# A recorded four-layer kernel played in another order: new tables of issue order, copy engines and buffer places

## The chip, the cores and the metric

The kernel runs on one core of a Trainium2 chip as one program. The metric is the device time of one execution in microseconds (us), as the median of several runs. The engines are TensorE (PE, matrix products; its weight loads are listed as PEld), VectorE (DVE), ScalarE (ACT), GpSimd (POOL) and SyncE (SP, which issues plain transfers). Each works through its own instructions strictly in order and waits for the others at semaphores.

## The reference

The input `x` is 2 batches x 1024 tokens x 128 channels in float32. Four layers follow, and each does the same around two functions of its own:

```python
xn = _layernorm(x, axis=-1)
s = _L0_attn_ref(xn, ...)
g = _silu(_L0_ffn_ref(xn, ...))
x = x + s * g          # then layers 1, 2 and 3 in the same way
```

- Layer 0: a delta rule in chunks of 32 tokens (a recurrence over a state, `next` in the kernel), two causal convolutions of `v` with 7 and 25 taps (`local`, `mid`, made of `conv` operations), and a router that mixes four such outputs (`mixed`); the other function is a chain of ternary linear maps with gelu.
- Layer 1: attention of 16 heads over all 1024 tokens, with a score made from distances (`sim`, `e`, `av`); the other function is a mixture of 8 experts of which each token uses 2.
- Layer 2: linear attention with 16 heads of 64; the other is a small transformer block on the eighth of the tokens that a router picks.
- Layer 3: causal attention of 16 heads with one shared key and value; the other is two blocks of attention in windows of 64 tokens with a gated map behind each (`g`, `a`, `u`, `down`).

## The kernel before

The stage functions (`l0_attn` L802, `l0_ffn` L1139, `l1_attn` L1171, `l1_ffn` L1335, `l2_attn` L1514, `l2_ffn` L1616, `l3_attn` L1823, `l3_ffn` L1982) do not issue anything. Their calls go to a recorder (`Record`, `note` and `product`, L472-L545), for layer after layer and batch after batch (`program`, L2234). The recorder makes 6,968 *units*, numbered in the order of recording. A unit is one operation of DVE, ACT, POOL or SP, or up to 32 matrix products of one tile shape on PE. Each unit knows which units must come before it. Copies that empty a PSUM bank (`evac`, L703) may run on ACT or on DVE; there are 426.

When all is recorded, `Record.order` (L547) decodes the table `ORDER` (from L308): a permutation of the unit numbers, with one bit in each that says whether a copy goes to DVE. `Record.issue` (L563) plays the units in that order. Each unit goes to the end of its engine's instruction stream, so the table fixes the order on every engine, PE's and the transfers' included. Where a unit first touches a tile, the tile gets a buffer: the next byte of the table `PLACES` says which place of its pool. There are 35 places of 128x1048 (`halves`, used by arrays such as `pr`, `mixed`, `xn`, and by the experts' weights `we`), 21 of 128x512 (`t512`, used by `e`, `xg`, `q`, `k`), 14 small ones, and 8 PSUM banks. A tile that takes a place waits until the last user of the tile before it is done. The two tables were computed elsewhere; the constants beside them (`LOAD`, `SHIFT`, `SEEN`) and the costs in `note` and `product` are not used when the kernel is built, except to give a unit its engine.

All engine calls are made on one line:

```python
for u, e in order:
    for b in u.buffers:
        if b.real is None:
            b.real = b.make(None if b.bufs is None else next(places))
    for op, args, kw in u.ops:
        if op == "evac":
            op = "copy" if e == ACT else "tensor_copy"
        f = getattr(engines[e], op)
        tc.keep_in_program_order(f(*map(real, args), **{k: real(v) for k, v in kw.items()}))
```

That is why every row of the profile says L584; groups are told apart by the names of their tiles.

The experts of layer 1 (L1335 and on, `gather` L1446, `fetch` L1455) need a word more. For each batch, tokens are sorted by expert into 23 tiles of 128 rows. POOL gathers the rows of each tile by an indirect transfer (`xg<-xd,token`), four tiles to a place of `t512`, and the expert's weights of each tile by another (`we<-in_experts,expert`), one to a place of `halves`. PE transposes the four parts of an `xg` (`tr<-const,xg`), multiplies by the weights (`up`, gelu on ACT, `down`), and POOL gathers the results back into token order (`y0`, `y1`). The indices `token`, `expert` and `slots` come from DVE.

Of the kernel before, what the change touches and what calls it, by code (L numbers as in the profile page):

```python
# [22 lines left out]
X = mybir.AxisListType.X  # L23
PSUM = bass.MemoryType.PSUM

P = 128
NB = 2
L = 1024
T = NB * L
# [240 lines left out]
def pack_inputs(inputs):  # L270
# [29 lines left out]
PE, ACT, DVE, POOL, SP = range(5)  # L300
# [8 lines left out]
    "c-nPZ2VfLM_rEu@ySI0jo)AJpOMuWJ0RjQ(h|(2l0s@~3A6?|bO3MK@M6rNMl@5Y{g@Ay7G=U%piF86q2%#h){qAymJM*8}-7Dey{-@q;nR)Z(z2AH9_a?"  # L309
    "5XIS2uSKb9`c`U3zksDRNK^2`Hx5c?p7VD>EbJpA)qTt37;Iv)RgK?#7{{11B!1HSGdg%;xImrnn54;sdYl>&s6J61Fsw+foMV&Le|hIgzLP`fnxOnls)L"  # L310
    "5pB`(D|G2GMkwE_>Xqw06}1`U62nTwzv#U9>3EP-p-2^b45g>i-I12q$GR{Ip0p5?<_EP%Z?Ughvj~qoER&;fyzT_lsIb&!o$hm<f9~vE`$DQ4)CxR{QsZ"
    "nZT|-N$|jZtxo{h(cN^aO32sgc(cbkr&`%W0#Eucgf1!Q(D<I}xeR7YOkB0Q$N4|u((O_G}M&&}1=UEVY<LA!~9)ZCrDN^?njqZB3z{+V3SpRND>I-0VeQ"
    "SN=+fgw4)9+@e9$EB!7IHaZ@(SB4suM!$hP*Kq9zgow7Vwt*A=5T9I+id0fPdew-RlUz%|x%hcPm;mceGzEH-Q_@Z&qJzbOp5pxZL7eQ@9{E1BfaDh$se!"
    "EsRY)3UT7KfsX*9pC@~vBokT#SWmPY3OoO9yKU6aWk*MWbg1{%(dzcm2T~#lz=4K|&=1!93t$<*OR`|C3RyWS2=#{-6S5B|dzT)lyApPx`Cncp?{8rXHM$"
    "V|)4|W*LI<+p$Ae_bH|tu!rSTac9iC}^{jN}FEu1UJeE+w8OzrgO0%$QF4t`m`M$s4ZAnVPZqxfzb-{9Y(M+DT}1Baxq(d_5oWS65wP4NBL+sIt8bk^7KP"
    "VDVQP*D);nZ2at4d>&;`T#$oq3|1X(4E|Pd?O~PE}S4V5=tVeFtLXF$*T9CtVx7FamUSL;6&F!dtl0U9L9TM^6F$q^~7WcKr^V9`!o~|^=4m#e>Uz8^a*!"
    ")Y}@BwX?_j5j!r(m(=)Pd8%T<r1ZyT}1HQw%=&-GV3P);ostR_900Kannvx}U0XW^+Gjd8~c?h(;86O02zMTu?GXfFn&zVuR{Eb40b{2x!UF+*<bzpkfl&"
    "Ym;rM2(W&gu&AFEwQN)<p|l!&BZFo&s-9XaV=?LaxnK8%l}e^DlHPGdSFkJdL0;oSZR@L&IF>Ftds~uF!e6**~oq9_l4NfJ$U_TA?%qT}-~1%m#(g0;>v7"
    "B7vcUBC7-bi4TUX)>)>MbHFep0g-+SYY%4uYL~e@QDqTvn4%u=!)U>=e!~9#P-2tq*7Elxvx>~{9+5Cn1v5(xf<wR{FhgMMHKp4lWwjPar4>1C0BH2jLYe"
    "kl8u(K=Ad!+$$Ya|!40a9OTIW6pxo?r5*xT?5Y=w$EBmfc3&apq6OKqYX4}g#2%%RYaBG`l!5MdN-9StyfCEe))D>%%VNyoBD^QCWgUor6|*aTyCxZ#!O-"  # L320
    "pLt%gh1IraoLexeC3@m)X;4k9yz+rOpF!0*-a%}3R6k<>4mf=qRl2+0S2bSxbPgQ4xv?;mP%pDGCc#1GkfS4vzBrRQ)2`bJ&K+?N1&9tVxgeE1K<h70-^="
    "*-ltTRs4S?TzokZ&M$!^9wNMYGc-v%502M_cx?*U}C*c-Ad36TEW?3m<0UL^u%p^O4iGWmBu-Ymp_zwa-9*2~(wXGh7890=r+YkmqT^$7T=?*Hx8yk!O2S"
    "E7UPmys|Cr^A~7t~wK)^yr1d-_t&F^f$gFy?D`V|^8($Z2(kvwf6=3bVc>Ws(IUq0$0m$7oDkQdB9y5d?@EIc&rVm_7jrEd)q~k9+huYK}yRIsrNUX)EGz"
    "mSH1GH+6!hq0nb1QS0Z`$q_MO=m^G8X`v(pIlxM=Lm&@pjfPjY{8}7|w)Qofk(<=Lr^Z8ptIwYIzw5KxA`1?6$cEmBh_j9$ta<-rB7xYP6gQkIsEsJbRe("
    "HEOk-LSDHKC6cMGN-9ENWtpj#35n&(8YUGaZszkaJNoQK}X>{6|w3gMexFC-C2ExQUHc&3b@i#dYhl~}l*LX`|ikwAU-3lhWP8io*38HVUIyi{aPc{X*9)"
    "gwBX3Dp4r1#>=$#AUsY(XUuC%_xHNr#t=jSxkP!PrHV~i(8>4JX+Ml)%zqm49$K!*_H-NC!k&46=%H!^Y6oct6d+Wv*san&*1Oxd^jaP9n6*R)iKy%0r(l"
    "tc*dV_x{KiJej`e+yRCP{rtiLbrd6t7=`tkeTs;hCN?3w{6@W|MVgbPPRV@zjjrw=ep>acq`Ai@bh2$Y1pPXR1k*OQ?=o9$k!DyR2Jrt>nks_4I^Glh19J"
    "LrI-T@f0``w5VaMgPtzz5{QhtL>DJ6VF53}1nIxj|HA2t0Xb*t3&X3V@omhAjsKk`h%Gv|#&ERqTr_4<>I#LA?$>f6!&w(mR|u<%YKtuQa(Id#AxeR3&*>"
    "P9m^w`^!_yg&vYamB;LaBhWKFvWoVUp)aB#<9i?Gz5;v-w`c}&Cm6+W23H|W1x(sNCT1B4{%#9r#QoiDh;64b7&m}hl`^<HUl54Hf<pKALk}Se1>LXxkj0"
    "_M0wo$AGY3Mp6v?(PKM1K3s3*9}13^ed8z(dHKM7;0>Pcu>EytStf3g#9joA6p!$;YZHbp+}oB1FqGm9a<iU+$YnK2m#KZrzNA~3bFOsKk|(6O$V9)l(bw"  # L330
    "Y=2w0%C4s`3ICJX7o}pTU~6?a>*0K%!>h~KnALeG=m~N4ym$M)`7bJnyxUoMKj#N;}CE{3}Z);9*WF_-cKsZOUnEf-fA>yzJuiv1i=WYK~NB_I)e!<i?#g"
    "TO+>$UdsqVsSO_$Odu0(&teRP5dn9V9QeM-d{zs2GX1fQ0NHHil?h)H}-@hRbYzk%>NHJ4ZrFIXZYquR?i93DZ>7<>buTBcAfyEKKhw$HFVQXyb&6h5`c="
    "U126J5{3YjCxfx`N0cjufPi;gy5W*MsTHOE*3kvpVSC;3{qU3DkPrqVI{^UXP$wCM2JQv;9R6d^Q6h;hRfo@b{g$$$*-`*K45V{P<ttxm*#R=?im1H;!XQ"
    "h`-zDv!k$j3ydy@hD%?7Z)3u@EFRltBn<c%8W8nf?O^rQ`<i|>M-Wt4S<3qd+5qjp^)}4i>fX6`jTt)!A1w=AyXhOL=Hr87BEFt+wb^p{^=q+V4`LqeFu}"
    "-lC&AsCU2Rq{05YyX%^%l|Wh7@StXc=P9-bN_(vHx2W=vmL8c{QJ((-PnVf9vMxah?{JO4Z)aYhs9obH(b%V&%j4xJ>(EW}|+0Kp@69ESpU7S0#<$htT#i"
    "}bJDga$Ft0_4<YMC%B{QRI`zq!`!_LJKgn5XU{?TFNg&9+|;$QjB#xzZDoQO1)l?5^>~34+v`XFAcZX|33FLkkuc-!=E5E86shkeLq7pO32?j_~%gvA??u"
    "yW`|viz;YVi__72kDC$uhQYV(ctLq~c%?B6<^^jeZDvnsrbaX;*sWlEQ3+=_i(KBhKGz6?}vnTWjXI*~{%bEFQPbEL@5q3u|g9&G|20e+)Ki4_(S9oppCf"
    "EW8J3+}6Mu;}RMme<j4lBKxgUfBdPF!{LQ}}#%{r!D^ZFOB0s{XKN42KK#A?~{u@-hegG~o|;w)?zPxD;0>V*?C^o`1b|ed2rjC#-43$OgPwV?#%1JUhDJ"
    "8_yUav<6&*8Jkd4$gPBPGazKqa@c%kUKu2AksUSmz}(CNs4=7huCt5;whw2$3vgoKVkaX>p=Hgltb-4i%~D`5+e({#wc31Pb2#hQ3@^!sPPKN!h&^vCw!("
    "mhTRVQaeCjMvm^XT5B1fmiJ;WRszo&DZS^uG^63%uw4Cms?rflhq!qBZ+V7=Ae1y^n4VOUeRey1L4vb#s_Ll&ov(BF?@djebpD0+TJa(u#@({rGq5`X$G)"  # L340
    "T&6%Od|0xm8k`Likh_&YUV~;G_aoirDnW*_xT+6Oc>wDleD>4;p?!pK!)KV=>w0WK|kgOU1(<#=0d^3rjMunyH#l1?W&vLv_9z;17|0$?3$W>dgJS;=%)c"
    "m@GxiXXSENl{iY%T5`L*wCm+{HZ}8f>*E0T|vNb!xJQ)^1^Bc1PzBEr|PPz?_OC4f9d#Me}2gCEhmJdG<gdgAd+Ftzi0%6Qn^4PNC(I*v4Zo;?0G}t+<)`"
    "w>IzZ#;VS@McSE@|Ee-CGg7q{@CNG5f&FU%`k@41Di9ze!IYp*G81CM<!Ok_Xo%E(@9lV7Is;D!`2CJu?kOU5@rio-(#K%<JQ%Q(K2kg#FW=Z0iB4oCueT"
    "PkaP3AEFg-eVse{{j0xpJF)PC4cVujIduTv#cLMA9A>Xc5Q_zPd)!8V*T08alhYQ0XY}Tk;wp=<H*bsEe7zYx`YqlXJ|c`T_(QL5^dkblXV3i4yAj1Uklt"
    "Phhv~p@Op5E>iYu&xTnP_cD{C;X*`PA=$s{;B{}oq@+pT_tPIub$gl9g_VayKNy;uNWeXN!hT7x73TW<sW3Gi8V)?l{nzl7`tn>V1sU&a@%zVanwj-yUzU"
    "U@l(4&0mYj|~bfuIm7+j%tdt&o=;9Shoo+z7HDl1Ea7s7vhJqUg1a7!20@(2QVFAWz~%2HDGBu89@RsRQZ>s?n5Tcer2`$)$ji$ZmtY*TS!Up((hnm^G?m"
    "~EMIX7dCq|~40u7PS$EgaeWMY*iE`atb8`Sv!cjq#>-he@jgiGgirA16@bt`TT@J-p1@N@AmR*ygY8D2W8P1>7ddO@`E+sywXiJ0gAl&VGl5!rP>4S!i&!"
    "t?rJ#&BmeF|w~srgGsbPvwqHRy$(M@TUE*Mhb<w;428-lQ;yw#W=Aw%|VLI7qc1T5DHojf$312DA%0+2t6<G%2V3ep^#=r}jgl*0U(QXr>KF!dL6bR|yuI"
    "WGCcQn481pyc%aa$gE9f^c6S3gvA_O>snY7>Teu*vM1b(KbePjLw9Iw>2w5T*WDhe-s{m8Ls5hL$_TiO%}!ZRVm9{@;$*jsD|Vn)5GL6J)!ihxHOU+e&O4"
    "+bqVJ%In3zLkY9VhrS54|HHIe1omJPUg#wBEP$_lI3i|4<+?S2eM>-WuH)@g+K)>jY@cic!uf+Dk=-re)YtYt1qt_qdsz&!hJ$0uz}$%spIRX&*rP;(hN6"  # L350
    "M{*R9FHcmWLn|EvSORw@<LFJkn2HBa|ChfmivN4Z`tx?xykge+!n^CTOPK7Oe>-Wm;QdXL*GZ)`6z7I%~QxZ=K4QDgVup<@S-t?N9X=U2jyRCc`j34v_~$"
    "oy2H921X>F19>ulU3;oYNin%SiC<?E%R*tBEBfbBqw01ewo0&2=9dF0Oe_S~pQUKL&f8f#8Bs0mt$?^AVHx56>Qd^644O0$PGOCpdJuRV!O5F@mFNS~CAv"
    "ZN+%$+|+<#sz&6n#BnB1}iL#iM%?c>%$lz0>!S=v3I}kec8oO<@UbB;0ANfTYG2Uv3<FRDR|NPP*QXbphp<z5q{NR=MmPv+Xa|?$x)^)3z$v6O<&E<G;;q"
    "seq2Z8b?1$+aYJ+dHWh|!Z_^?uJ>C7>$VjzA4Cbz2r3I8KAmx|r0dAh?;!j-X0w(;`^xzO9dNGK-Y^H*(}A_7LUO&f;=Sw7*$#D*4^S*t1XqQcUBo7<(wD"
    "QAqM>qPEdEo*d2-KUFgt8+Ai-y3+)(ydopJebCDaq$AMJ9&2u3GPBia$sP}cTultawY!<W-jg}<aEP*_7>b{RE03=rKh!+~l;47v=>Pjr)=s!iTc>KDkVf"
    "1vJXJYd5m5{CAdTVVP3uHgE!wH$mh^+M7qfdRa+<*)XP>0!vb$E?nNqphqlhxLiJwGC6w6%|k0`hpTtZY>LSNTDtv3tE+XLc=Rdg}TL_hjGEzBO>K0dA&R"
    "FCKiy=@>cnTs-3UHeL#ChA7^a1lYH-bOEt1s-ik(A4lfwhxYp(9l=EHSKu{HuP&slj?j=Oajk>Oj_&J&)(IUE0r*nDMj8{V8T*gS2op5L#khmLp!*kI+To"
    "GMJTRFnvTz7t!FyzSrxByVv9!jO+7~w=iMja&?xhxqH-VCdU3|c=@tb6lzpM%Y!a$Zd%iEhCv0pt7%u|)hm`FD7!<m0Z_rfj(T=CYvnhq{+rpIwpQ2(GwO"
    "()n@=Qlt6d(g@N|krc^!qR(%ILk!-D=<fi};X}Rmr-VPKxi6^8F$H5!&?yvF9BI9nT>tT@8lCSZXHNbWo&OB5`&vS9MW`D*cIPriA58?a7LGJyWa0p*y*v"
    "khJGOZAD-FJX{UdI7*f@@LdyqD1<r|CN661=|zdvQ|`VI&lHhw0{*jFy1QuM-$kXw61;-vc4FD6V~JAKKBCCv-Z{orWorNzH7#<k$1<>suH;Yt`PW=|?F7"  # L360
    "X7|_5=^5l8$BwAp5R$9zI%>xKf6)((H;$tjDEPWX+M50H|03O$UOnx+z1)0tun*za;SX@x`CVJpe;ck%?M6)S!+E5kp8x~@Q*{n=Tko>v&|o>;q8v2%6^B"
    ";)K(;ssIoc$j;7bxl*$`R)`NmdtgOp{u_vK(D_FIbbw{g)EowSqUg6f!RkIeqbMeyH<&ol?k6^BCCERz6X#6oVGx{WTLfU9#-U$Es!W~B*zDK`+xtrTH#@"
# [1971 lines left out]
```

## Time and profile before

| what | value |
|---|---|
| time, median of 3 runs | 1747.01 us (1742.27, 1747.01, 1753.01) |
| the profiled execution's own time | 1748.91 us |
| its span, from the first to the last instruction | 1747.2 us, mean granted PE clock 0.976 |
| a copy of 128x512 on ACT, on DVE | 593, 682 ns |
| products of 128x512, start to start | 429 ns, 522 where the tile shape changes |
| indirect gathers on POOL (`xg`, `we`) | 46 and 46, 1005 and 949 ns each |

The profile is one execution. The digits of its slices are tenths of busy time in 40 equal slices of the span, and PEclk the tenths of the full clock that PE was granted. Rows of the waits give the idle time of an engine and what ended it: total, number and the longest. Rows of the timeline give start and duration, engine, operation, out<-in, count, and in brackets the idle time just before with its releaser. Rows of the windows give, for each stretch, the busy time and the instructions of PE, PEld, DVE, ACT and POOL, the granted clock, the DMA share and GB/s.

"PE work" in the text is a position on PE: the sum of the products' streaming time from the start of the order, 1466 us in all.

### The profile page before, as it was taken

How to read it: one execution, taken by the hardware profiler on the slowest of the kernel's cores; microseconds unless marked ns; L12 is line 12 of the kernel's file. 1: busy time of each engine (PE TensorE's matmuls, PEld its weight loads, DVE VectorE, ACT ScalarE, POOL GpSimd, SP SyncE). 2: the span in 40 equal slices, each digit the busy share in tenths (PEclk: the TensorE clock that was granted, in tenths of full speed). 3: DMA queues.
4: the chain of work that ended last, by engine and by line, in shares of the span. 5: the costliest groups of instructions: out<-in, count | busy, mean ns of one | idle time of the engine just before them, and what ended most of it. 6: DMA issues, size and time to landing. Idle time of an engine off the chain costs nothing.

```text
span 1747.2 us, 35516 instructions
## 1 busy us (share of the span) xinstructions
PE 1633.7 (94%) x14112; PEld 902.7 (52%) x14112; DVE 1208.8 (69%) x2377; ACT 996.6 (57%) x1770; POOL 569.0 (33%) x732
## 2 busy tenths in 40 slices
PE   6999998879999998999999899899999998999996
PEld 3565446643335732367565468544346664443383
DVE  6874886682314442175999998778788988866764
ACT  3222422238998698964555565565555665656542
POOL 1020011032232255112101670656535654952301
PEclk9998999888999999999999999999999999999998
DMA  3110011002223324143031134312005323010130
GB/s 124 22 20 3 1 25 27 15 2 88 82 65 93 101 62 117 18 146 106 13 112 36 59 84 127 101 32 66 5 23 135 96 70 104 18 46 28 26 115 24
DMA packets 96055, 106.23 MB, mean 61 GB/s; under 512 B 50225, under 2 KB 62513, under 8 KB 95761
## 3 DMA queue, kind: packets, MB, share of 16 engines
q1 hardware_dynamic: 86608, 74.11, 15.4%
q0 software_dynamic: 9280, 29.86, 5.8%
q8 instruction: 111, 1.82, 0.4%
q14 instruction: 56, 0.45, 0.1%
HBM read 87.24 MB, written 8.29 MB: 55 GB/s over the span
## 4 chain that ended last, share of the span: by engine, by line
PE 59%; DVE 24%; issue 5%; POOL 5%; ACT 4%; DMA 2%; SPq 1%; DVEq 0%; ACTq 0%; POOLq 0%
PE sim L584 13%; PE av L584 6%; DVE e L584 5%; PE tr L584 4%; PE num L584 3%; PE wo L584 3%; PE down L584 3%; DVE conv L584 3%; DVE u L584 2%; PE up L584 2%; PE ph L584 2%; ACT e L584 2%; POOL e L584 2%; PE p L584 2%; DVE j L584 2%
## 5 line engine op out<-in xcount | busy, mean ns | idle before, releaser
L584 ACT ACTIVATE e<-sim,own 128x512 f32<-128x512 f32 x512 | 303.5, 710 | 21.3 <-PE sim L584 12.5
L584 ACT ACTIVATE e<-sim 128x512 f32<-128x512 f32 (+3 forms) x384 | 166.7, 498 | 97.8 <-PE sim L584 34.2
L584 DVE TENSOR_TENSOR e<-e 128x512 f32<-128x512 f32 (+3 forms) x320 | 166.6, 555 | 55.7 <-PE num L584 29.9
L584 PE MATMUL num<-e,v 128*64 128x64 f32 (+4 forms) x1280 | 165.2, 384 | 3.4 <-POOL e L584 2.6
L584 POOL TENSOR_SCALAR_AFFINE_SELECT e<-e 128x128 f32<-128x128 f32 x256 | 116.4, 486 | 149.7 <-ACT e L584 141.1
L584 PE MATMUL sim<-qT,k 32*128 32x512 f32 x1024 | 157.9, 644 | 4.5 <-DVE k L584 3.3
L584 PE MATMUL sim<-q,kT 64*128 64x512 f32 (+3 forms) x768 | 149.1, 513 | 11.0 <-ACT e L584 8.8
L584 PE MATMUL av<-e,va 128*32 128x512 f32 x1024 | 133.6, 615 | 0.6 <-ACT e L584 0.6
L584 PEld LDWEIGHTS num<-e,v 128*64 128x64 f32 x1280 | 78.4, 137 | 86.6 <-issue 53.0
L584 POOL TENSOR_TENSOR sq<-qk,tab 128x256 f32<-128x256 f32 x128 | 105.1, 844 | 45.5 <-DVE ss L584 27.0
L584 PE MATMUL ph<-h,w_f 128*128 128x512 f32 x256 | 115.9, 604 | 3.1 <-DVE ko L584 2.1
L584 PEld LDWEIGHTS sim<-q,kT 64*128 64x128 f32 x768 | 61.7, 185 | 98.9 <-ACT e L584 65.4
L584 PEld LDWEIGHTS sim<-qT,k 32*128 32x128 f32 x1024 | 48.7, 185 | 97.7 <-ACT e L584 72.0
L584 POOL DMA_INDIRECT xg<-xd,token x46 | 46.2, 1005 | 146.4 <-ACT e L584 122.3
L584 POOL TENSOR_TENSOR u<-u,sq 128x512 f32<-128x512 f32 x64 | 85.7, 1349 | 2.3 <-DVE last L584 0.2
L584 ACT ACT_TABLE_LOAD x45 | 57.7, 1283 | 49.4 <-DVE lg L584 11.1
L584 PEld LDWEIGHTS ph<-h,w_f 128*128 128x128 f32 x256 | 48.0, 193 | 59.7 <-issue 54.4
L584 DVE SCALAR_TENSOR_TENSOR conv<-vT,w_a,conv 128x1024 f32<-128x1024 f32 x60 | 77.7, 1297 | 1.5
L584 ACT ACTIVATE e<-e 128x512 f32<-128x512 f32 x96 | 57.5, 626 | 26.0 <-DVE e L584 24.6
L584 PE MATMUL qk<-w_f,shifted 128*128 128x512 f32 x128 | 62.0, 609 | 8.7 <-ACT kT L584 2.8
L584 ACT ACTIVATE h<-ph,w_f 128x512 f32<-128x512 f32 x32 | 21.8, 688 | 84.7 <-PE ph L584 78.1
L584 PEld LDWEIGHTS av<-e,va 128*32 128x32 f32 x1024 | 23.7, 109 | 82.2 <-issue 69.6
(545 smaller groups left out, 3413.9 us busy)
## 6 DMA issues: line engine op xcount, KB each, us to landing
zb<-zd SPq DMA_DIRECT2D x192, 128.0 KB
rb<-rd SPq DMA_DIRECT2D x64, 128.0 KB
w<-v SPq DMA_DIRECT2D x60, 128.0 KB
tab<-in_rotary SPq DMA_DIRECT2D x8, 512.0 KB
yd<-y SPq DMA_DIRECT2D x10, 256.0 KB
w_f<-in_f SPq DMA_DIRECT2D x4, 512.0 KB
w_l<-in_l SPq DMA_DIRECT2D x4, 512.0 KB
w_f<-in_f SPq DMA_DIRECT2D x4, 448.0 KB
```

Of the source, the lines that this page charges most:

```text
L584: tc.keep_in_program_order(f(*map(real, args), **{k: real(v) for k, v in kw.items()}))
```

## The change

Only the two tables differ; no line of code does. The diff is 258 lines of which all but the frame are encoded text:

```diff
 ORDER = (
-    "c-nPZ2VfLM_rEu@ySI0jo)AJpOMuWJ0RjQ(h|(2l0s@~3A6?|bO3MK@M6rNMl@5Y{g@Ay7G=U%piF86q2%#h){qAymJM*8}-7Dey{-@q;nR)Z(z2AH9_a?"
...
 PLACES = (
...
+    "j=2Y1@$m(v|=Qm>!$+*<BLirH#7|<aiF!1ucWqhFJ3o*Y@Fm6e0>1k`X3PbcW("
 )
```

Decoded, the units, their dependencies and their number on each engine are the same (PE 1598 units, SP 604, POOL 728), but for copies: 212 stay on ACT and 54 on DVE, 81 go from DVE to ACT and 79 from ACT to DVE, most of them `q`, `qT`, `qk`, `kT` and `z` of layer 3. ACT then has 335 plain copies for 333, DVE 207 for 209.

What moves, by the position of a unit on its own engine:

- PE: 947 of 1598 units are displaced by more than 0.5 us of PE work, 391 by more than 2, 51 by more than 10, most of them in the first 300 us and in layer 1. The order is unchanged at 285 to 320 us of PE work, where layer 0 hands over to layer 1, and in the last 34 us. Changes of tile shape between successive units are 537 for 534. Runs of narrow products (32x32 and 64x64, up to 64 columns) that last over 2 us sum to 55.3 us for 53.7, and are 16 for 15.
- DVE: the median unit is displaced by 3.0 us of DVE work, 525 by more than 5. ACT: 2.7 us, 145 by more than 5. SP: hardly.
- Semaphore waits in the program: 7910 for 7907.

The places in the order that the prediction speaks of (unit numbers after #):

```
POOL, gathers of layer 1, batch 1
before: xg#2476 (place freed by PE av#2083), xg 2440 2474 2439 2526 2442 2524 2500 2477 2441,
        we#2545, xg 2452, we 2471, xg 2449, we 2522, xg#2475, ...
after:  ... xg 2500 2502 2474, xg#2439 (place freed by PE av#2083), we 2522, xg 2452 2499 2501 2475,
        we 2495 2547, xg#2476 2477, ...
PE:     tr#2493 needs xg 2474 to 2477; it stands at 547.5 us of PE work before, 545.3 after;
        tr#2518 needs xg 2499 to 2502; 564.2 before, 544.9 after
POOL, hand-over of layer 0 to layer 1
before: par, va1, par, rank, pr, pr, pr, va0, xg#1725, ln_r, ln_r, before, we#1747, we ...
after:  we#1723 (needs DVE expert#1663), par, par, va1, pr, pr, pr, we#1720, we#1696, va0, rank, ln_r, ln_r, xg ...
DVE, place in its order, before and after
        ko#100 121 -> 34;  mixed#439 284 -> 270 and nn#634, nn#631 283, 285 -> 289, 291
        expert#1663 632 -> 552, slots#1645 615 -> 541, token#1657 594 -> 600
        k#1143 596 -> 597: before, cT, token and mixed#972 stand ahead of it; after, they stand behind it or on ACT
        v1#6432: copy on DVE before, on ACT after
```

The first 388 us of PE work have 13 gathers of batch 0 ordered ahead of them before, and 20 after.

## The prediction

> **What bounds the kernel now.** The page comes first, because it says which engine sets the time.
>
> ```profile
> PE 1633.7 (94%) x14112; PEld 902.7 (52%) x14112; DVE 1208.8 (69%) x2377; ACT 996.6 (57%) x1770; POOL 569.0 (33%) x732
> ...
> PE   6999998879999998999999899899999998999996
> ...
> DVE  6874886682314442175999998778788988866764
> ...
> PEclk9998999888999999999999999999999999999998
> ...
> PE 59%; DVE 24%; issue 5%; POOL 5%; ACT 4%; DMA 2%; SPq 1%; DVEq 0%; ACTq 0%; POOLq 0%
> ```
>
> PE is busy for 1633.7 of 1747.2 us. The change alters no product, so what it can win is small: the 113.5 us in which PE is idle (1747.2 - 1633.7), the time added where the clock was granted at half, and switches between tile shapes. The chain still gives DVE 24%: where DVE is the fuller engine its queue decides when PE goes on. The windows of 100 us show where that is.
>
> ```profile
> 300.00:400.00 100.00, 86.59 (x1300) 56.38 (x1299) 70.25 (x233) 37.46 (x56) 25.16 (x22) 0.88 0.03 8
> 400.00:500.00 100.00, 99.37 (x721) 33.48 (x718) 28.34 (x98) 94.47 (x162) 32.60 (x38) 0.97 0.29 91
> ...
> 600.00:700.00 100.00, 95.05 (x712) 34.62 (x712) 33.56 (x56) 90.25 (x150) 48.98 (x49) 0.97 0.33 94
> ...
> 900.00:1000.00 100.00, 91.09 (x442) 54.94 (x441) 95.65 (x196) 57.75 (x96) 33.20 (x34) 0.95 0.20 61
> ...
> 1400.00:1500.00 100.00, 90.37 (x683) 53.15 (x681) 82.19 (x144) 61.74 (x112) 52.35 (x52) 1.00 0.27 76
> ```
>
> In 300-400 the clock is 0.88 and PE idles 13 us; in 900-1000 DVE is 95.65% busy and PE idles 9 us; in 1400-1500 PE idles 10 us. In 400-700 it is ACT that is full (94.47 and 90.25). The last view is PE's waits by releaser.
>
> ```profile
> PE tr L584 <- DVE xn L584: 15.8, 3, 13.5
> ...
> PE tr L584 <- DMA xg<-xd,token: 5.0, 1, 5.0
> ...
> PE sim L584 <- DVE k L584: 3.3, 1, 3.3
> ...
> PE qk L584 <- DVE k L584: 2.5, 1, 2.5
> ...
> PE ph L584 <- DVE ko L584: 2.1, 1, 2.1
> ...
> PE num L584 <- DVE v L584: 1.6, 1, 1.6
> ```
>
> All waits in that list are short and scattered; the largest, on `xn`, is mostly the 13.5 us of the first load and normalisation, which no order removes. One wait on a transfer stands out (5.0 us, once), and the timeline shows its cause:
>
> ```profile
> 669.46 0.95 POOL L584 DMA_INDIRECT xg<-xd,token  x1 [13.74 <-ACT e L584]
> ...
> 688.62 0.94 POOL L584 DMA_INDIRECT xg<-xd,token  x1 [0.30 <-issue]
> ...
> 692.18 0.90 PE L584 MATMUL tr<-const,xg 128*128 128x128 f32 x3 [4.95 <-DMA xg<-xd,token]
> ```
>
> Between 669.46 and 692.37 POOL issues 19 gathers, 1.25 us from start to start; PE's transposes of `xg` began at 686.90 and stood 4.95 us for one of them.
>
> **The change, part by part.** Both programs hold the same 6,968 units; only order, places and 160 engines of copies differ. So each part is a wait that goes or comes.
>
> *Gathers of layer 1, batch 1.* Before, the burst opens with gather 2476, which takes the place of an `e` tile that PE's `av` frees at about 669.4; gather 2475, needed by the same transposes, stands 15 issues later: 669.46 + 15 x 1.25 = 688.2 (the trace has 688.62), and the data is there 3.6 us later, at 692.18. After, the gather that takes that place is 2439; 2477, the last that these transposes need, is 9 issues behind it: 669.5 + 9 x 1.25 = 680.8, plus 3.6 is 684.4. The transposes stand within 2.2 us of PE work of where they stood (686.9), and those of the neighbouring group now come right ahead of them. I therefore take 5.0 us away. Bounds: 0 if the release comes later by as much, and -6.5 with half of the slow stretch behind it (4.12 us at clock 0.50 in the windows below, of which at most half can be saved).
>
> ```profile
> 686.00:692.18 6.18, 1.23 (x10) 0.28 (x4) 0.00 (x0) 3.26 (x6) 4.72 (x5) 0.78 0.74 214
> 692.18:696.30 4.12, 4.12 (x19) 1.22 (x19) 0.69 (x1) 0.69 (x1) 3.02 (x4) 0.50 0.65 177
> ```
>
> *Gathers of batch 0.* They start earlier: 20 instead of 13 are ordered ahead of 388 us of PE work. They share POOL with the `pr` products and the masks. One in 300-400 took 1.96 us beside DVE's `mixed`, against 0.95 elsewhere; seven more at the difference of 1.0 are 7 us of POOL, which is 25% busy there. Nothing waits for them within 1 us by the same count as above, so 0; what they could do if they wait themselves is the second rival.
>
> [...]
>
> *Layer 0, first batch (90-120 us).* PE waited 2.11 us at 96.65 for `ko`, which stood 120 instructions deep in DVE behind the `prod`/`u` solve, and 1.30 us at 118.48 for `vk` behind three `conv` of 1.28. `ko` now stands at place 34 of DVE. But other releases moved back (another `ko` now is released after 80 us of DVE work, needed at 79.5 us of PE work), so the two are not simply gone. I added DVE's measured durations up to each unit PE needs, less PE's work up to there (429 ns per pass of 512 columns): the peak of this lead was 2.4 us at 80-100 us of PE work and is now 0.4. So -2.0; bounds -3.4 (both waits) and +1.0 (from the row `vk`, a new one of like size).
>
> *`mixed` ahead of `nn` (221 us).* Before, PE waited 2.28 us for `nn` behind `mixed`, 3.01 us.
>
> ```profile
> 221.25 3.01 DVE L584 TENSOR_TENSOR mixed<-local,lg 128x1024 f32<-128x1024 f32 x1
> ...
> 224.51 0.66 PE L584 MATMUL tr<-const,vT 128*128 128x128 f32 x4 [2.28 <-DVE nn L584]
> ```
>
> Now `mixed` stands ahead of both `nn` that PE's next banks need, but PE has one 3.4 us `ph` more before the transposes that use them. I take +1.0; bounds -2.3 and +3.0.
>
> *Hand-over from layer 0 to 1 (300-400 us).* PE's order is the same here. On DVE the routing of layer 1 (`expert`, `slots`, `token` are units 1663, 1645, 1657) moves forward by up to 80 instructions. The lead at 300-320 us of PE work rises from 12.1 to 14.1: +2.0, bounds 0 and +4. In turn `k` at 382.86 loses `mixed` (2.01), `cT` (0.67) and others, 3.1 us ahead of it, and gets 1.1: -2.0, bounds -3.3 (the wait in the list) and 0.
>
> *Layers 2 and 3 (900-1500 us).* DVE's work ahead of what PE needs was 130.4 us below PE's at 1020 us of PE work and is 135.9 below now; at 1240 it was 104.0 and is 108.9, so about 5 us of DVE work have moved behind the units PE waits for. Here PE waits of 2.6 (`pg` for `kf`), 2.5 (`qk` for `k`), 2.96 (`pkv` for `u`), 1.98, 0.85 and 1.05 us (the last three at 1105 to 1113) lie on DVE rows, 11.9 in all. I take -4; bounds -8 and 0, the upper because `turn` and `shifted` (3.1 us) have joined ahead of one release at 964.
>
> *`v` and the copies.* The 1.59 us before `num` at 1388.88 came from a copy of `v` on DVE behind small ops of 0.65; that copy is now on ACT. With 2.8 us of `ln` sums taken out ahead of `u` at 1390: -2.5, bounds -3.0 and 0. Of the others as many copies go one way as the other (81 to ACT, 79 to DVE; 593 against 682 ns): 2 x 0.68 us of DVE, beside PE: 0.
>
> *What comes new.* Most units move (DVE's by a median of 3.0 us of DVE work, ACT's by 2.7), so waits must come that no row can show: I take one of the size of those named above, +2.5; bounds 0 and +15 (about all named gains). Three more switches of shape at 93 ns (522 against 429 ns): +0.3. Runs of narrow products over 2 us long: 53.7 to 55.3 us, 16 of them for 15; a slow stretch of 3.41 us costs at most 1.7, and I take +0.5.
>
> *Tail.* PE's last 34 us of work keep their order, so the 4.09, 0.92 and 2.35 us waits stay: 0, bounds -1 and +1.
>
> Sum: -5.0 - 2.0 + 1.0 + 2.0 - 2.0 - 4.0 - 2.5 + 2.5 + 0.3 + 0.5 = -9.2 us. The profiled execution took 1748.91 (span 1747.2 and 1.7 around it), so it would take 1739.7; that run lies 1.9 above the median of 1747.01, so the median should be 1737.8, and I say 1738.
>
> **The rivals.**
>
> *As many new waits as old ones.* The engine sequences change at thousands of places and PE stays at its 1634 us; if the new waits reach the 12 us of gains, the time is 1747. For it: 40 waits of about 0.5 us in layers 0 and 3 gain neighbours as often as they lose them. Against it: the 5 us gather wait has a cause that is gone.
>
> *A gather that blocks POOL at the hand-over.* In the new order a `we` gather stands ahead of `par` and of the three `pr` products of batch 1, and it waits for `expert` from DVE. Before, it came after them. If `expert` is late, POOL stands and with it `pr`, `mixed` and what PE needs at 350-400, where waits of 1.1, 1.2, 3.4, 2.4, 3.0 and 2.5 us (13.6) already lie. It decides from about 9 us of lateness on, which uses up the gains. Price: those waits doubled, +13.6, and two slow stretches more, +3.4; less 9.2 this ends at 1747.0 - 9.2 + 17 = 1755, and with no other gain at 1764. For it: DVE is the fuller queue there. Against: POOL is 75% idle there, and `expert` is ahead in DVE too.
>
> *The slow stretches go with the waits.* The mean clock of 0.976 makes 2 x 0.024 x 1747 = 84 us at half, which cost up to 42. If the waits at 221, 380-399, 687, 964 and 993 go entirely and seven stretches with them, 7 x 1.7 = 12 more are won, and the layer 2/3 term reaches -8: 1738 - 12 - 4 = 1722. Against it: most of those stretches follow narrow products, whose runs did not get shorter.
>
> [...]
>
> **How the numbers follow.** Likeliest case (about 1738, its own range 1727 to 1745): 0.43. As many new waits: 0.25, 1745 to 1755. Blocked POOL or another queue: 0.16, 1753 to 1775. Slow stretches too: 0.16, 1715 to 1729. Runs of one kernel differ by 10.7 us (1742.27 to 1753.01), so about 1% (17 us) is what a measurement can tell from no change. Faster by over 1% (under 1729.5): the last case and a quarter of the first, 0.27. Slower by over 1% (over 1764.5): the upper half of the blocked queue and a little more, 0.12. Within: 0.61. The range takes in the second case, most of the third and most of the fourth: 1718 to 1761.
>
> **What would show it.** Right: no PE wait on the `xg` transfer, and clock 1.00 near 690; no PE wait on `ko` or `v`; PE busy unchanged near 1634 with idle down by about 9; 900-1200 fuller. Wrong: a POOL queue that stands at the first `we` with `pr` behind it; PE idle over 15 us in 300-400; a new wait of over 3 us on a place; granted clock below 0.97. If ACT's full stretch at 400-500 or 600-700 now empties PE, a cause that I did not cost was at work.

## The result, and the profile after

The changed kernel takes 1731.22 us (median of 6 runs, 1727.87 to 1734.38) against 1745.95 for the kernel before (6 runs, 1742.09 to 1753.01): a ratio of 0.9915, 95% interval 0.9888 to 0.9941. That is 14.7 us, inside the predicted range and 6.8 us below the predicted 1738. The profiled execution took 1734.35 us (span 1732.6, mean clock 0.973) against 1748.91 (1747.2, 0.976), 14.6 us less. The total agrees fairly with the forecast (range 1718 to 1761); its parts, as will be seen, do not, so that much of the agreement is luck.

The page of the changed kernel:

```profile
PE 1624.5 (94%) x14112; PEld 909.6 (53%) x14112; DVE 1203.7 (69%) x2375; ACT 991.9 (57%) x1772; POOL 560.9 (32%) x732
...
PE   6999988887999999999998999899999998999996
...
DVE  4994878386211724425899999768788998967865
...
PEclk9999999798999999999999999999999999999998
...
PE 54%; DVE 29%; issue 7%; ACT 4%; POOL 2%; DMA 2%; SPq 2%; DVEq 0%; ACTq 0%; POOLq 0%
```

Two things show at once: in the clock row the eighth slice (303 to 347 us) fell from 8 to 7, and the chain's share of DVE rose from 24% to 29%. PE's busy time, which was to stay at 1634, is 9.2 us less. No product has gone, so part of what was won lies inside "busy" time: this profile models the ends of the matmuls, and the group `sim<-q,kT` of layer 3 alone went from 149.1 to 142.4 us for the same 768 products. So the split into busy and idle is no test here; time at equal PE work is.

The windows of the changed kernel (columns as before: PE, PEld, DVE, ACT, POOL, clock, DMA share, GB/s):

```profile
300.00:400.00 100.00, 84.48 (x1326) 56.69 (x1326) 64.44 (x213) 29.31 (x44) 28.29 (x20) 0.84 0.09 27
400.00:500.00 100.00, 95.08 (x670) 37.16 (x668) 35.07 (x103) 89.52 (x154) 17.16 (x22) 0.94 0.16 48
...
600.00:700.00 100.00, 98.23 (x764) 43.95 (x763) 36.26 (x65) 91.44 (x147) 43.16 (x43) 1.00 0.34 100
...
900.00:1000.00 100.00, 92.95 (x487) 56.61 (x487) 96.05 (x206) 57.53 (x94) 29.28 (x32) 0.98 0.18 54
...
1400.00:1500.00 100.00, 93.37 (x692) 55.69 (x690) 85.85 (x153) 56.73 (x105) 51.44 (x57) 0.97 0.27 76
```

600-700, 900-1000 and 1400-1500 are fuller; 300-400 is emptier (PE idles 15.5 us instead of 13.4) and slower (0.84 for 0.88). In 400-500 the drop is mostly a shift: the hand-over now ends later.

PE's waits by releaser in the changed kernel:

```profile
PE tr L584 <- DVE xn L584: 15.2, 4, 13.7
PE sim L584 <- ACT e L584: 8.6, 14, 1.6
...
PE pu L584 <- DVE mT L584: 3.8, 1, 3.8
PE sim L584 <- DVE k L584: 3.7, 1, 3.7
...
PE w L584 <- DVE ko L584: 2.5, 1, 2.5
...
PE kk L584 <- DVE ka L584: 2.1, 1, 2.1
```

The wait on `xg` is gone and so is the one on `v`. The waits on `ko` and `k` are still there, and `mT` and `ka` are new.

To see where the time went, both traces are laid over each other by position on PE: for each amount of PE work done, the time of the one less the time of the other. It is worked out from the start times of PE's units in the two profiled executions. PE work here is streaming time alone, 1439.6 us in all; the 1466 us given with the kernel before counts 0.1 us more for each of 264 units of small products.

| PE work done, us | time before, us | after less before, us |
|---|---|---|
| 125 | 166.0 | -1.6 |
| 175 | 216.7 | -1.2 |
| 225 | 274.4 | +7.0 |
| 250 | 309.2 | +3.6 |
| 300 | 390.3 | +14.1 |
| 525 | 659.5 | +16.0 |
| 550 | 697.0 | +8.9 |
| 600 | 756.8 | +11.1 |
| 825 | 1014.5 | +3.7 |
| 900 | 1096.4 | +4.6 |
| 1100 | 1331.7 | +0.8 |
| 1300 | 1568.7 | -8.1 |
| 1400 | 1682.3 | -10.1 |
| 1437 (PE's last unit) | 1736.7 | -14.3 |

So there are three parts: layer 0 and the hand-over *lose* 14 to 16 us, layer 1 from 525 on wins 12.3 (+16.0 to +3.7), and layers 2 and 3 from 900 on win 18.9 (+4.6 to -14.3). The net 14.3 is what is left of some 31 won. Units that were reordered make single points uncertain by a few us. Each trace is one run besides, and the runs differ by 6.5 us for the changed kernel and by 10.9 for the kernel before, so a stretch is firm where several traces agree on it.

### The profile page after: what moved, and what is told of

The parts are those of the page before. It is cut to its first block, busy times and chain, and to the rows that moved or that the text cites. A ratio compares the mean times of both kernels' runs of the same rounds, so it can differ in the third digit from the quotient of the medians.

```text
span 1732.6 us, 35482 instructions
## 1 busy us (share of the span) xinstructions
PE 1624.5 (94%) x14112; PEld 909.6 (53%) x14112; DVE 1203.7 (69%) x2375; ACT 991.9 (57%) x1772; POOL 560.9 (32%) x732
## 4 chain that ended last, share of the span: by engine, by line
PE 54%; DVE 29%; issue 7%; ACT 4%; POOL 2%; DMA 2%; SPq 2%; DVEq 0%; ACTq 0%; POOLq 0%
PE sim L584 13%; PE av L584 6%; DVE e L584 5%; PE tr L584 4%; PE num L584 3%; PE down L584 3%; DVE u L584 3%; PE up L584 3%; PE ph L584 2%; DVE conv L584 2%; PE wo L584 2%; PE pu L584 2%; SPq L584 2%; DVE qf L584 1%; DVE acc L584 1%
## 5 line engine op out<-in xcount | busy, mean ns | idle before, releaser
L584 PE MATMUL sim<-q,kT 64*128 64x512 f32 (+3 forms) x768 | 142.4, 505 | 7.2 <-ACT e L584 6.6
L584 PE MATMUL av<-e,va 128*32 128x512 f32 x1024 | 130.0, 602 | 0.7 <-ACT e L584 0.7
L584 POOL TENSOR_TENSOR sq<-qk,tab 128x256 f32<-128x256 f32 x128 | 99.7, 800 | 44.8 <-DVE ss L584 32.9
L584 POOL DMA_INDIRECT we<-in_experts,expert x46 | 45.8, 995 | 152.8 <-DVE row L584 65.2
L584 POOL TENSOR_SCALAR ln_r<-ln_v 128x8 f32<-128x8 f32 x12 | 3.9, 323 | 242.2 <-DVE ln_v L584 242.2
```

## The experiments

The programs can be cut and joined because the units are the same in both. In each experiment only the two tables were rebuilt, so the code is the same and its line is L582 or L583. Where a cut separates units of which one order has some already and the other not, those go right behind the cut. The table above is the reading to be tested: the hand-over loses, the gathers win some 7, layers 2 and 3 win by their own order, engines or places. Each expectation names its own theories A and B.

**e1_old_start: the hand-over's loss, undone.**

```diff
-order(after), all units
+order(before) up to 360 us of PE work, then order(after); 34 units cross the cut, 17 tiles get other places
```

> The order, copy engines and places of before up to 360 us of PE work, then the order and copy engines of the changed kernel (34 of 6,968 units lie on the other side of the cut, none of them on PE; 17 tiles take another place than in either). By the two traces the changed kernel reaches 300 us of PE work 14 us later than before and wins 28 us after that. Theory A, each stretch keeps what it lost or won: 1731 - 14 = 1717 us, 0.983 to 0.984 of before. Theory B, the early routing and gathers of the new start pay for the later gain: no better than the changed kernel, 1731 or more (0.991 and up).

Measured: 1728.81 us (6 runs; before 1747.16 in the same job), ratio 0.9892 [0.9858, 0.9927]: between the two. At 300 us of PE work it stands at +2.6, not +14.1, so before's start does avoid the loss; but at 525 it is at +14.2. The join gave 11.6 us back in layer 1. The waits of PE show on what (the list is of the whole run):

```profile
PE sim L583 <- ACT e L583: 10.5, 15, 1.4
PE up L583 <- DMA we<-in_experts,expert: 2.3, 2, 1.8
...
PE tr L583 <- DMA xg<-xd,token: 0.9, 1, 0.9
```

The changed order has gathers of batch 0 ahead of 360 which the order before has behind it; joined there, they come late, and neither wait on a transfer exists in the changed kernel. From 475 to 675 us these two, the waits for `e` (2.1) and one more (1.2) sum to 6.5 us, and 10.2 us at half clock (0.87 on average from 640 to 680) cost up to 5.1 besides, an estimate. So a bad seam hid the answer in the total, and the stretch up to 300 gave it: the loss belongs to the changed order up to 360. That the early gathers of the new start do not have to be paid for by it is shown only by e5 below.

**e2_old_end: without the gain of layers 2 and 3.**

```diff
-order(after), all units
+order(after) up to 900 us of PE work, then order(before)
```

> The changed kernel up to 900 us of PE work, then the order, copy engines and places of before (14 units on the other side of the cut, none on PE). By the traces the changed kernel is 4.6 us behind at this point. Theory A, the gain in layer 3 belongs to the order of that stretch: 1746 + 4.6 = 1751 us (1.003 of before). Theory B, the gain comes from the state that is handed on (places, work of DVE already done): it stays in part, below 1742.

Measured: 1748.73 us (10 runs), ratio 1.0012 [0.9994, 1.0030], as theory A had it. From 900 to the end it stays between +2.4 and +5.1 us. The whole gain behind 900 is that stretch's own, and what is ahead of 900 is, alone, worth nothing or less.

**e3_gathers_only: one part alone, on the kernel before.** Only three gathers of POOL move:

```diff
-xg#2476, xg 2440 2474 2439 2526 2442 2524 2500 2477 2441, we 2545, ... xg 2475
+xg#2476 2474 2477 2475, xg 2440 2439 2526 2442 2524 2500 2441, we 2545, ...
```

> The kernel before with one thing changed: the gathers 2474, 2477 and 2475 follow directly on 2476 in POOL's queue, so that the four parts that PE transposes first are issued first (the last of them at about 669.5 + 3 x 1.25 = 673.3 us, and landed by 677 for a use at 687). Theory A, the wait was the place in the queue: 5 to 7 us less than before, 1740 (0.996 to 0.997). Theory B, the wait is covered by another (ACT is 90% busy there, and PE waits for its e next): 1744 to 1746 (0.999 to 1.000).

Measured: 1737.59 us (11 runs), ratio 0.9952 [0.9934, 0.9969], 9.6 us less. In its profiled execution PE's time falls by 7.0 us between 525 and 550 us of PE work and by 5.1 more between 600 and 825. The 7.0 are the wait (4.95) and the slow stretch behind it (4.12 at half, so 2.06). What stood there at clock 0.50 now reads:

```profile
686.00:692.00 6.00, 6.00 (x48) 1.74 (x50) 0.69 (x1) 6.00 (x11) 4.61 (x5) 1.00 0.78 225
692.00:697.00 5.00, 5.00 (x36) 1.95 (x32) 1.24 (x3) 4.87 (x10) 3.08 (x5) 1.00 0.81 247
```

PE is full and the clock 1.00. The later 5.1 us, which no theory had, are not the gathers': from 600 to 825 PE's waits of this trace and of before's are the same to 0.4 us, but before's has four slow stretches there (13.7 us at half clock, mean clock 0.97) and e3's none (1.00; from 900 to 1000 us on the clock 1.00 for 0.95). With before's order and without the moved gathers, e7 and e11 take 254.9 us for this work, before's trace 257.7 and e3's 252.5. So part of the 12 us by position is the one trace of the kernel before, and the same holds for the 7.4 us that the changed kernel (250.2) wins there.

**e4_old_copies and e7_new_copies: the engines of layer 3's copies.** 107 copies of layer 3 change engine, in the changed kernel back to what they were, and in the kernel before to what they become.

```diff
-copies of l3_attn, l3_ffn on the engines of their own ORDER
+copies of l3_attn, l3_ffn on the engines of the other ORDER (e4: after's order, e7: before's)
```

> The changed kernel, with order and places as they are, but the copies of layer 3 on the engines that before had them on (107 of them change: 51 to ACT, 56 to DVE). Theory A, the choice of engine carries the gain of layer 3 (18 us from 900 us of PE work on): most of it goes, 1743 to 1749. Theory B, the order and the places carry it: 1731 to 1734, for 5 more copies of 0.68 us on DVE.

> The kernel before, its order and places as they are, with the copies of layer 3 on the engines that the changed kernel has them on (107 change). Theory A, the new engines are the better ones: 1735 to 1744. Theory B, an order and its engines belong together, and each set of engines with the other's order loses (the fourth experiment lost 51 us against the changed kernel): 1765 to 1800 (1.01 to 1.03).

Measured: e4 1782.18 us (4 runs), ratio 1.0204 [1.0172, 1.0237]; e7 1780.24 (4 runs), 1.0190 [1.0166, 1.0214], as its theory B had it. e4 fits neither theory: the mixture is worse than both kernels, by 51 us against the changed one. It loses steadily from 825 us of PE work on. e7 answers it from the other side, 35 us over the kernel before. The waits of PE from 960 us to the end, e4 first:

```profile
PE sim L582 <- DVE q L582: 11.1, 4, 3.8
PE tr L582 <- DVE kk L582: 5.7, 1, 5.7
```

and the same stretch of e7:

```profile
PE sim L582 <- ACT e L582: 9.2, 14, 2.1
PE sim L582 <- DVE q L582: 7.9, 5, 3.1
...
PE sim L582 <- DVE qT L582: 4.8, 2, 2.7
```

In the kernel before, `sim` waited 1.6 us for `q` there. These rows are the largest, not the whole loss; by them copies are late on the engine that the order did not reckon with. So the new engines have no worth of their own: order and engines are one fit.

**e5_joined: the two gains put together.** e3's order up to a point where the sets of issued units nearly agree, then the changed one.

```diff
-order(after), all units
+order(e3) up to 760 us of PE work, then order(after); 6 units cross the cut, no tile gets another place
```

> The kernel before with the gathers 2474, 2477, 2475 put forward, up to 760 us of PE work; from there the changed kernel's order, copy engines and places (6 units on the other side of the cut, none on PE; no tile takes another place). Theory A, layer 0 lost and the stretch from layer 2 on won, each for itself: 1747 - 10 (the gathers) - 22.7 (the changed kernel from 760 us of PE work on, 8.4 behind to 14.3 ahead) = 1714 us, 0.981 of before. Theory B, time won early is given back at the join as in the first experiment (which got 2 to 3 us of 14): 1725 or more, 0.987 and up.

Measured: 1714.84 us (5 runs, 1711.01 to 1721.22), ratio 0.9818 [0.9792, 0.9844] to the kernel before, and its whole interval lies below the changed kernel's 0.9888 to 0.9941. In its profile it is at +0.2 at 300, -6.7 at 550, -10.3 at 800 and -31.6 at the end. This is theory A, and it confirms the reading of the table: the 14 us are lost ahead of 360, and the changed order from 760 on wins its own (24.9 us here, 22.6 in the changed kernel) without the early start. Its page:

```profile
PE 1619.7 (94%) x14112; PEld 899.3 (52%) x14112; DVE 1199.6 (70%) x2373; ACT 993.3 (58%) x1772; POOL 562.4 (33%) x732
...
PE   6999998888999999999999999899999998999996
...
PEclk9998999998999999999999999999999999999998
```

PE idles 95.6 us (1715.3 - 1619.7) where it idled 108.1 in the changed kernel, and the eighth digit of the clock is 9 where that has 7 and the kernel before 8.

**e6_one_copy: the copy of `mT`.** The change put one copy of layer 0 on DVE, behind nine `conv`.

```diff
-mT#462: DVE
+mT#462: ACT
```

> The changed kernel with one copy put back: unit 462, a copy of mT out of a PSUM bank at 276 us, goes to ACT again. In the changed kernel it stands on DVE behind nine conv (11.84 us) and PE waits 3.8 us for its bank. Theory A, the wait is the copy's place: 3 to 4 us less than the changed kernel, 1727.5 to 1728.5 (0.989 to 0.990 of before). Theory B, DVE's queue is full there and PE waits for the next unit of it instead: 1731 (0.9915).

Measured: 1728.29 us (6 runs), ratio 0.9888 [0.9865, 0.9912]. The value is as expected, 3 us below the changed kernel, but the intervals overlap. The traces are firmer. The changed kernel's DVE:

```profile
264.03 11.84 DVE L584 SCALAR_TENSOR_TENSOR conv<-vT,w_a,conv 128x1024 f32<-128x1024 f32 x9
275.79 0.68 DVE L584 COPY mT<-tr 128x512 f32<-128x512 f32 x1
```

The input of the copy was ready at 260.21; on ACT it runs at 259.75 in e6's trace and the 3.8 us wait of `pu` for `mT` is gone. By position e6 is at +1.3 at 225 where the changed kernel is at +7.0, yet at +12.1 at 300: most of the early gain does not last through the hand-over.

**e8_other_places, e12_large_places and e11_before_places: the table of places.** The order and the engines stay; from 900 us of PE work on, each new tile takes the place that has been idle longest in the order. e8 does so for 128x1048, 128x512 and small places (817 tiles change place), e12 for all but the 128x512 (220 tiles), e11 does what e8 does to the kernel before.

```diff
-place = next byte of PLACES
+place = the one, of those free at this point of the order, whose last user is earliest
```

> The changed kernel with other places from 900 us of PE work on: each new tile of the three large SBUF pools takes the free place that has been idle longest in the order (817 tiles get another place; the PSUM banks and all orders stay). Theory A, order and engines carry the gain and the SBUF places hardly matter: 1731 within 3 us (0.990 to 0.993). Theory B, the table of places was fitted to the order and carries part of it: 1736 or more (0.994 and up).

> As the eighth experiment, but only the pools of 128x1048 and of the small tiles are dealt anew; the 128x512 tiles (e, z, q) keep the changed kernel's places. Theory A, the 14 us of the eighth came from the e tiles of attention, whose places ACT waits for: 1731 within 3 us (0.990 to 0.993). Theory B, they came from the large tiles, by loads of SP that wait for a place at the head of its queue: 1740 or more (0.996 and up).

> The kernel before with other places from 900 us of PE work on, dealt as in the eighth experiment (the free place that has been idle longest in the order). Theory A, the old table of places fits the old order as the new one fits the new: about 14 us more than before, 1755 to 1765 (1.006 to 1.011). Theory B, the old places were no better than such a rule, and the change's gain in layer 3 came from a better table: within 4 us of before (0.998 to 1.002).

Measured: e8 1745.63 us (10 runs), ratio 0.9991 [0.9972, 1.0010]: all 14 us are gone, with the changed order and its engines untouched. e12, e11 and two more below ran on another chip, where the kernel before took 1819.81 us (19 runs), so that only their ratios can be compared: e12 0.9862 [0.9816, 0.9908], e11 1.0009 [0.9983, 1.0035]. The changed kernel itself was not run on that chip, but the positions hang less on that: from 900 us of PE work to the end e12 wins 18.1 us, the changed kernel 18.9 and e8 only 8.1. So the large and small places alone carry nothing; the 128x512 places do, by themselves or with the others. And the kernel before loses nothing with its places dealt by the simple rule (theory B of e11): its table was not better than that. One stall in e8's trace shows how a place can cost time:

```profile
1634.99 1.67 ACT L582 ACTIVATE e<-sim 128x512 f32<-128x512 f32 x3 [0.30 <-PE sim L582]
...
1641.95 1.46 ACT L582 ACTIVATE e<-sim 128x512 f32<-128x512 f32 x3 [2.07 <-DVE e L582]
...
1642.60 3.84 PE L582 MATMUL sim<-q,kT 64*128 64x512 f32 x10 [2.17 <-ACT e L582]
```

The `e` at 1641.95 had its data at 1634.90, but its place still held another `e` that DVE finished at 1641.92; ACT stood, its PSUM bank stayed full, and `sim` stood for it. `sim` waits 13.8 us for ACT's `e` in e8 from 1090 us on, and 6.6 in the changed kernel. How much of these 7.2 us goes back to places in this way is not taken apart.

**e9_window_all and e10_window_not_pe: is it the window of 250 to 300?** The 342 units that the changed kernel has at 250 to 300 us of PE work are put in the order before, all of them, or all but PE's.

```diff
-units at 250 to 300 us of PE work in order(after)
+the same units in order(before)   (e10: PE's stay in order(after))
```

> The changed kernel, but its 342 units between 250 and 300 us of PE work stand in the order of before, on all engines (12 copies on before's engines, 41 tiles in another place). In this window the changed kernel loses 8 to 10.5 us. Theory A, the loss is made in this window and by the orders in it: 8 to 10 us less than the changed kernel, 1721 to 1723 (0.985 to 0.987 of before). Theory B, as in the first experiment the time comes back in layer 1: 1728 to 1731 (0.989 to 0.992).

> The same window in the order of before, but PE keeps the changed kernel's order in it (so the product wk that feeds a chain of small sums stays 14 us of PE work later, and the wide products stand as thinly between the narrow ones, where the clock was 0.50 to 0.67 against 0.73 to 0.96). Theory A, DVE and ACT, with the routing ahead of the sums, made the loss: as good as the kernel with all engines put back, 1721 to 1723. Theory B, PE's own order made it, by the late product and the slow clock: little is won, 1728 or more (0.989 and up).

Measured, against the kernel before on that other chip: e9 0.9870 [0.9832, 0.9908], e10 0.9919 [0.9889, 0.9949]. e9's ratio is what theory A asked for, but that does not carry it: e12, whose start is the changed kernel's own, stands at 0.9862 on the same chip. By position e9 is 1.3 us below the changed kernel's first trace at 300, and e12 is 1.5 below, so nothing is won. That does not clear the order inside this window, for e9 loses its time in another way. From 250 to 275 us of PE work PE was busy 35.9 us in the kernel before and 42.8 in the changed kernel, and idle 4.5 and 4.9; in e9 it is busy 36.1 and idle 8.3. The slow stretch at 330 is gone,

```profile
330.00:340.00 10.00, 8.06 (x257) 6.63 (x252) 4.29 (x19) 3.28 (x5) 0.00 (x0) 1.00 0.01 3
340.00:350.00 10.00, 10.00 (x204) 9.13 (x204) 7.11 (x25) 4.94 (x5) 0.07 (x1) 0.66 0.01 3
```

and a wait is there that neither kernel has:

```profile
PE feat L582 <- DVE uw L582: 3.4, 1, 3.4
```

e10, with PE's order of the changed kernel, has both, a clock of 0.67 and 0.50 at 330 to 350 and 3.4 us for `uw`, and is worse (+8.9 at 300 against the changed kernel; its theory B): again two orders that do not fit each other. So the slow stretch goes with PE's order in this window. Whether putting the window back would win without new waits at its edges, no run here shows.

## Why the prediction was right, and where it was wrong

The sum was -9.2 us and the profiled executions show -14.6. The two largest misses, 10.5 us at the hand-over and 12.4 the other way in layers 2 and 3, nearly cancelled, and it is by this luck that the total came so close.

*Gathers of layer 1, batch 1: right, too small.* Predicted -5.0 (0 to -6.5); between 525 and 550 it is -7.1 in the changed kernel, and -7.0 in e3 where nothing else moves, a little beyond the bound. The count of nine issues of 1.25 us held, from a later start because all came later:

```profile
685.14 0.94 POOL L584 DMA_INDIRECT xg<-xd,token  x1 [10.72 <-ACT e L584]
...
696.47 0.95 POOL L584 DMA_INDIRECT xg<-xd,token  x1 [0.30 <-issue]
```

685.14 + 9 x 1.25 = 696.39. The transposes follow without a wait at 699.47, and PE's clock is 1.00 from 686 to 701. The mis-sized term is the slow stretch, of which I allowed half: it went whole.

*Layer 0, first batch: about right in size, wrong in which wait goes.* Predicted -2.0; from 75 to 125 us of PE work it is -1.9. But `ko` did not stop being late: PE waited 2.50 us for another `ko` at 102.38. `vk` (1.3) went, and with it 0.8 us of waits for `silu` and `state`.

*`mixed` ahead of `nn`: right in sign.* The 2.3 us for `nn` went, and between 200 and 250 us on the clock 2.1 us for `ka` and 2.4 that end in "issue" came. Predicted +1.0; these sum to +2.2. Whether moving `mixed` alone does this was not tried.

*Copies beside PE at 0: wrong.* "2 x 0.68 us of DVE, beside PE: 0" counted the durations, and not where in its queue each copy went. One of the 79 went behind 11.84 us of `conv`: a wait of 3.8 us, 3 us in the median (e6, intervals overlapping). The waits that come new were put at +2.5; this one and `ka` alone are 5.9.

*Hand-over: this step failed.* Predicted 0 (+2.0 for the lead of DVE's queue, -2.0 for `k`); from 250 to 300 us of PE work it is +10.5, and +9 to +15 at 300 in all six traces that have the changed start. Its first sentence, "PE's order is the same here", holds only from 285 us of PE work on, which is 362 us on the clock. From 243 to 285, which is 300 to 362 us, 45 of 77 units of PE move by more than 0.5 us, and `wk#1088` from 261.4 to 275.7; 8.3 of the 10.5 us are lost by 285. The lead of DVE's queue was the wrong measure besides: DVE was emptier there (64.44 us in 300-400 for 70.25), and the wait on `k` stayed (3.7 us). The rise of this lead from 12.1 to 14.1 does not come out either: with DVE's times of the profile before and 0.68 us for each copy that comes to it, the lead goes to some 17. What the traces show in its place is slow PE work first and a late chain behind it. In the changed kernel

```profile
330.00:340.00 10.00, 9.20 (x138) 7.88 (x127) 2.21 (x10) 0.93 (x2) 0.00 (x0) 0.50 0.01 2
340.00:350.00 10.00, 9.37 (x201) 8.10 (x202) 4.45 (x12) 3.43 (x4) 0.00 (x0) 0.50 0.02 3
```

while in the kernel before

```profile
330.00:340.00 10.00, 9.69 (x239) 8.67 (x226) 5.53 (x17) 5.99 (x6) 0.00 (x0) 0.73 0.02 5
340.00:350.00 10.00, 10.00 (x57) 4.73 (x56) 9.58 (x37) 2.37 (x4) 0.00 (x0) 0.93 0.00 0
```

and in e5, which has before's start,

```profile
330.00:340.00 10.00, 9.38 (x302) 8.32 (x295) 5.86 (x19) 5.99 (x6) 0.00 (x0) 0.83 0.01 3
340.00:350.00 10.00, 9.48 (x57) 4.35 (x57) 9.61 (x36) 2.37 (x4) 0.00 (x0) 1.00 0.01 2
```

At 0.50 the wide products between the narrow ones take nearly twice as long (a group of eight `wk` 2.08 us at 331.70, for 1.16 in the kernel before at 330.13, ahead of its slow stretch). Between 250 and 275 us of PE work the time at half clock is 27.3 us in the changed kernel and 10.2 before. By estimate, half of the difference, that costs up to 8.5 us more, and the stretch takes 7.3 us longer, 6.9 of them with PE busy. The other 3.2 us come from 275 to 300 and are idle time: the routing's `sums` start at 371.46 instead of 357.85, and PE waits for `infx` (2.3), `place` (1.6) and `token` (1.3), none of which is a wait of the kernel before.

The slow stretch goes with PE's order. Between 250 and 275 the time at half is 24 to 27 us in e2, e6, e8, e10 and e12 and 17 in e4, which all have the changed order of PE there, and 3 to 10 in e1, e3, e5, e7, e9 and e11, which have before's (e9 but for one unit). The whole loss is that of the changed order up to 360 (e1, e5), but which units make it stays open: e9 puts `wk#1088` back at 261.4 with the rest of the window, its `sums` start at 366.97, and the time it saves on the clock it loses on new waits.

*Layers 2 and 3, and `v`: the step was mis-sized.* Predicted -4 and -2.5; it is -18.9 from 900 to the end. `v` did go (1.6 to 0). The count behind the -4, a lead of DVE that falls by some 5 us, does not come out: counted in the same way it rises, from -130.4 to about -126 at 1004 us of PE work. In the list of PE's waits from 960 us on the clock, these of the kernel before have gone, `num` but for 0.2:

```profile
PE pkv L584 <- DVE u L584: 3.0, 1, 3.0
PE qk L584 <- ACT kT L584: 2.8, 1, 2.8
PE num L584 <- POOL e L584: 2.6, 5, 0.9
PE qk L584 <- DVE k L584: 2.5, 1, 2.5
```

Only the first and the last were among those I counted; the other two lie on ACT and POOL, whose queues I had not followed in that stretch, and `pg` for `kf`, which I had counted, stayed (2.4). New ones came too (`tr` for `kk` 3.0, `qkv` for `vT` 2.2), and the whole list falls from 47.6 to 36.6 us. And the places were not costed at all, although the change rewrites their table: with an ordinary deal of places the same order and engines win nothing in all, and 8.1 of the 18.9 us from 900 on (e8). In the prediction "only order, places and 160 engines of copies differ" stands ahead of ten terms of which none is a place.

*The rivals.* The `we` gather at the hand-over did block POOL, for 65 us, and it cost next to nothing:

```profile
376.34 2.06 POOL L584 DMA_INDIRECT we<-in_experts,expert  x1 [65.16 <-DVE row L584]
378.43 5.82 POOL L584 TENSOR_TENSOR par<-par,const 1x16 f32<-1x16 f32 x2
```

The data of `par` was ready at 378.03, 0.4 us before POOL was free. A long wait of an engine says nothing until it is known when its next instruction could have run. The rival of slow stretches that go is half true: they went at 687, and came at 330 to 350; the mean clock fell from 0.976 to 0.973. "Most of those stretches follow narrow products" does not come out: of the 18 stretches at 0.50 in the kernel before (the one after PE's last product aside), 5 have mostly products of 32x32 or 64x64 in the 3.41 us ahead of them. As many new waits as old ones describes the first 900 us (e2: 1.0012), though not the end. Tail: predicted 0, -1 to +1; in the last 34 us of PE work it is -4.3. Two of the signs that were to show the forecast wrong came as well, a POOL queue that stands at the first `we` and PE idle over 15 us in 300-400 (15.5), and of those for right, idle down by about 9 did not (113.5 to 108.1): none of them settled the total.

On the clock, the windows of 320 to 350 us in the changed kernel have PE busy 8.14, 9.20 and 9.37 of 10 us, its longest idle from 300 to 350 is 1.14 us, and the clock is 0.67, 0.50 and 0.50. The trace has it at 0.50 without a break from 326.80 to 350.69, and in both traces the stretches at 0.50 last 3.41 us or two to seven times that, but for the one at the end. In the kernel before, the clock fell to 0.50 at 689.52, 2.3 us into the 4.95 us wait for `xg`; here no wait of PE is half as long. Most products from 320 to 350 are narrow (560 of 623 are 32x32); whether the clock fell for that, and with it whether there is ground for the +0.5 put down for narrow runs, no run here tells.

## What to carry to other kernels

Lay two orders over each other by work done on the bounding engine and read the difference stretch by stretch: a total inside the range hid 30 us won and 16 lost, and the same table showed where to cut for a version (e5, 0.9818) that keeps the one without the other. Order, the engines of copies and the buffer places of such a table are one fit: engines exchanged alone cost 35 to 51 us here, and places dealt anew 14 in the changed kernel and nothing in the kernel before, so whoever forecasts a new table must cost a place as a wait on the last user of the tile that held it. Count an issue queue one by one (nine gathers of 1.25 us were right to 0.1 us), and for each copy that changes engine look at what stands ahead of it there, not at its own duration.

## What the hardware showed that was not expected

On the chip of the last four experiments the kernel before took 1819.81 us instead of some 1746, and all four kernels of that job, whatever their tables, took 55 to 60 us more between 360 and 560 us of PE work than their counterparts elsewhere (e9, e10 and e12 against the changed kernel, e11 against the kernel before); in e9 POOL issues gathers back to back there, 19 from 644.01 to 666.51, 1.25 us from start to start. ACT stood there with its input ready. ACT's waits from 400 to 760 us in e12:

```profile
ACT e L582 <- remote: 38.6, 8, 13.6
ACT e L582 <- PE sim L582: 18.2, 22, 2.9
```

and one of them in its timeline:

```profile
673.28 4.74 ACT L582 ACTIVATE e<-sim,own 128x512 f32<-128x512 f32 x8 [13.59 <-remote]
```

"remote" is a release that the profile can't put down to an engine of this core; it occurs in these four traces and in none of the others. Once it starts, an `e` lasts as long as in the changed kernel (4.74 us for eight; 4.73 and 4.97 there). In e9 the data of such an `e` was there 8.5 us and its place 17.5 us before it ran. No run here shows what ACT waited for. The stretches by position up to 300 lie ahead of it; the ratios of that job carry it on both sides, if the kernel before, of which there is no trace there, has it too.
